# Token-routed attention block and expert layer: zero fill, one-hots, first block's root and third matrix moved within the prologue

## The chip, the cores and the metric

The kernel runs on one core of a Trainium2 chip. The metric is device time in microseconds (us), the median of three runs. Such a core has a matrix engine (TensorE, PE in the profile; its weight loads are shown as PEld), a vector engine (VectorE, DVE), a scalar engine (ScalarE, ACT), a programmable engine (GpSimd, POOL) and SyncE (SP), which in this kernel only issues transfers. Transfers run on 16 DMA engines; SyncE's go through queue q1, GpSimd's through queue q0.

## The reference

2048 tokens of 512 features pass through two layers. The first picks one of four 512x512 matrices by the token's number and uses that same matrix three times; the second is a mixture of 32 experts, of which every token takes four, with one shared expert.

```python
# first layer, xn = layernorm(x); C = ctx[e], e = token id // 6250
y   = (silu(xn @ C.T) * (xn @ C.T)) @ C
x   = x + y
# second layer
h   = rmsnorm(layernorm(x)) * norm_w
p   = top-4 of softmax(h @ gate_w.T), made to sum to 1
out = x + layernorm(x) + sum over the 4 experts of p * expert(h) + shared(h)
```

Both the expert and the shared path are `silu(h @ g) * (h @ u) @ d`. An expert holds at most 512 tokens.

## The kernel before

**Sorting the tokens.** The kernel first sorts the tokens by matrix, so that a block of 128 rows holds tokens of one matrix, or at a border is worked twice with a mask (`valid`). There are 16 blocks and up to 3 more at the borders (`XB` = 19). The sort is done with small matrix products: `ge` compares the token numbers with the borders (L226), `xm` is the membership (L229), and products with a triangular matrix count the ranks (L235 to L243). `split` cuts each token's place into block and row. Then, for each of 16 columns, `xa` is a one-hot of the row (L262), `xb16` is a one-hot of the block times the token's number (L253, L259), and 16 small matmuls add them up (L263). The result, `xtok` (L265), is the list of rows to gather. `planned` (L313) ends a chain of small VectorE instructions on which matrix each block uses.

**Gathering.** `x_block` (L332) is an indirect transfer that GpSimd issues, 128 rows of 2 KB each. GpSimd also computes the roots of the layer norm (`x_root`, L352, a power of -1/2), and the code ties its gathers and powers to a fixed order with `in_turn`: three gathers, then root 0, a gather, root 1, a gather, root 2, a gather, root 3, two gathers, the roots of blocks 4 to 7 in one, and eight gathers.

**One block.** VectorE takes mean and variance (`x_moments`, L344 and L345), GpSimd the root, VectorE two scalars (`x_norm`, L407 and L410), and ScalarE writes the normalised rows `hn` (L426). TensorE transposes them (`turn_block`), and the copy out of the accumulator is `xT`. `up` (L464) multiplies with the matrix, `gate` does silu(u)*u, and `down` (L485) multiplies with the same matrix again. For blocks after the first, `hold` (L395) lets ScalarE copy the block's matrix to a fixed place, because its number is known only at run time. TensorE's order in the steady part is: the next block's `up`, transposes of the block after, this block's `down`.

**The first block** is treated apart: VectorE and ScalarE each write half of `hn` (L416, L426), each half is transposed and copied by itself, and `up(0, ...)` goes by feature chunks, three before block 1's transposes and one behind. Idle matmuls (`turn_over`, L273) keep TensorE busy in the waits.

**Order.** The framework waits on data by itself; `behind` adds an order by hand, with a wait when it names `Sync`. `apart` states that two accesses don't touch. Every engine takes its own queue strictly in order. On VectorE the statistics of block 2 stand ahead of the copy `xT` of block 1, and those of block 3 ahead of block 0's gated product.

**Transfers from SyncE.** The token numbers, then three matrices of 1 MB (L111), the fourth after `planned`; behind the statistics of block 7 the weights of the second layer and 1 MB of zeros to the padding of the output (`second_inputs`, L133), and after the last gather 20.8 MB of blank rows to `s_dram` (L887). The zeros come from the tile `none` of 2084 columns, which GpSimd fills (L163) before writing an index into its last columns (L164).

The second layer (routing, scatter into `s_dram`, the experts' products, scatter into `out`) follows the first one's last blocks and is not touched.

Of the kernel before, what the change touches and what calls it, by code (L numbers as in the profile page):

```python
# [17 lines left out]
P = 128  # L18
T = 2048
D = 512  # L20
# [46 lines left out]
def tile_xattn_moe(  # L67
# [42 lines left out]
    def context(e):  # L110
        return nc.sync.dma_start(cT[:, e], ctxT[e].rearrange("(c p) f -> p c f", p=P))  # L111

    matrices = [context(e) for e in range(EX - 1)]
    gate_sb = const.tile([P, DC, E], F32, name="gate_sb")
    nw = const.tile([P, DC], F32, name="nw")
    nwq = const.tile([P, DC], F32, name="nwq")
# [31 lines left out]
    nc.vector.tensor_scalar(tri16, iota_q, row_b[:, 0:1], None, ALU.is_gt)  # L148
    iota16 = const.tile([P, P], F16, name="iota16")
    nc.vector.tensor_copy(iota16, iota_q)  # L150
    tok16 = const.tile([P, NT], F16, name="tok16")
    nc.vector.tensor_copy(tok16, tok1)
    ident = const.tile([P, P], F32, name="ident")
    at_hand = nc.vector.tensor_scalar(ident, iota_q, row_b[:, 0:1], None, ALU.is_equal)
    mhalf = const.tile([P, 2, GT], F32, name="mhalf")
# [4 lines left out]
    iota_e = const_iota([P, E], [[1, E]], "iota_e")  # L160

    spare = const_iota([P, NT, K], [[K * P, NT], [P, K]], "spare", base=NS, channel=1)
    nc.gpsimd.memset(none, 0.0)  # L163
# [60 lines left out]
    for e in range(1, EX):  # L224
# [20 lines left out]
    nc.vector.tensor_tensor(xv, px.rearrange("p (e t) -> p e t", e=EX), xm, ALU.mult)  # L245
    xrow = const.tile([P, NT], F32, name="xrow")
    nc.vector.tensor_reduce(xrow, xv.rearrange("p e t -> p t e"), AX.X, ALU.add)
    xblk, xq = split(xrow, ctx_pool, "x", F16)

    xa = ctx_pool.tile([P, NT, P], F16, name="xa")  # L250
    xbt = ctx_pool.tile([P, NT, NT], F16, name="xbt")
    xb16 = ctx_pool.tile([P, NT, NT], F16, name="xb16")
    nc.vector.tensor_tensor(  # L253
        xbt,
        iota16[:, :NT].unsqueeze(1).to_broadcast([P, NT, NT]),
        xblk.unsqueeze(2).to_broadcast([P, NT, NT]),
        ALU.is_equal,
    )
    nc.vector.tensor_tensor(xb16, xbt, tok16.unsqueeze(2).to_broadcast([P, NT, NT]), ALU.mult)  # L259
    pi = ps_s.tile([P, NT], F32, tag="sm", name="pi")  # L260
    for i in range(NT):
        nc.vector.tensor_scalar(xa[:, i, :], iota16, xq[:, i : i + 1], None, ALU.is_equal)  # L262
        nc.tensor.matmul(pi, xa[:, i, :], xb16[:, i, :], start=(i == 0), stop=(i == NT - 1))  # L263
    xtok = const.tile([P, NT], I32, name="xtok")
# [47 lines left out]
        nc.vector.scalar_tensor_tensor(valid, xw, xs_[:, e : e + 1], valid, ALU.is_ge, ALU.add)  # L312
    planned = nc.vector.tensor_tensor(valid, valid, be, ALU.is_equal)  # L313

    matrices.append(context(EX - 1))
    behind(matrices[-1], planned, mybir.DependencyClass.Sync)

# [49 lines left out]
    def x_registers(b):  # L367


        if b == 0:  # L370
            off[0] = 0
            regs[0] = 0, 0
            return None
        with queued(downs[-1] if downs else None):

            off[b] = nc.tensor.value_load(be_i[0:1, b : b + 1], min_val=0, max_val=min(b, EX - 1))
        with queued(adds_x[-1] if adds_x else halves[-1] if halves else None):
            dv = nc.vector.value_load(bl_i[0:1, b : b + 1], min_val=0, max_val=NT - 1)
            loaded = nc.cur_bb.bb.instructions[-1]
        with queued(reads[-1] if reads else None):  # L380
            ac = nc.scalar.value_load(bl_i[0:1, b : b + 1], min_val=0, max_val=NT - 1)
        regs[b] = dv, ac
        return loaded

    def hold(b):

        if b == 0:
            held[0] = cT[:, 0]
            return
        with queued(copies[-1] if copies else None):  # L390
            e = nc.scalar.value_load(be_i[0:1, b : b + 1], min_val=0, max_val=min(b, EX - 1))
        held[b] = ctx_pool.tile([P, DC, D], F32, tag="held", name=f"held{b}", bufs=2)
        n = DC // 2
        for h in range(0, DC, n):
            ins = nc.scalar.copy(  # L395
                held[b][:, h : h + n], cT[:, bass.ds(e, 1), h : h + n].rearrange("p o c f -> p (o c) f")
            )
            apart(ins, matrices[b + 1 :], "of experts that come later")
            copies.append(ins)

    def x_norm(b):
# [12 lines left out]
        n = D // 2 if b == 0 else 0  # L414
        if n:
            scaled = nc.vector.tensor_scalar(  # L416
                hn_[b][:, :n],
                acc[:, bass.ds(dv, 1), :n].rearrange("p o d -> p (o d)"),
                rv[:, 0:1],
                rv[:, 1:2],  # L420
                ALU.mult,
                ALU.add,
            )
            apart(scaled, loads[b + 1 :], "of blocks that come later")
            halves.append(scaled)
        ins = nc.scalar.activation(  # L426
            hn_[b][:, n:],
            acc[:, bass.ds(ac, 1), n:].rearrange("p o d -> p (o d)"),
            AF.Identity,
            bias=rv[:, 1:2],  # L430
            scale=rv[:, 0:1],
        )
# [26 lines left out]
    def up(b, fs, after_=None):  # L459
        if fs[0] == 0:  # L460
            ups[b] = ps_m.tile([P, DC, P], F32, tag="mm", name="pp")
        pairs = [(f, c) for f in fs for c in range(DC)] if b else [(f, c) for c in fs for f in range(DC)]
        for f, c in pairs:
            ins = nc.tensor.matmul(  # L464
                ups[b][:, f, :],
                held[b][:, c, f * P : (f + 1) * P],
                xT_[b][:, c, :],
                start=(f == 0 and c == 0) if b == 0 else (c == 0),
                stop=(c == DC - 1),
                skip_group_check=(b == 0),  # L470
            )
            if after_ is not None:
                behind(ins, after_)
        ups_.append(ins)

    def gate(b):
        s = xpool.tile([P, DC, P], F32, tag="s", name="s")
        gated.append(nc.scalar.activation(s, ups[b], AF.Silu))
        aT_[b] = xpool.tile([P, DC, P], F32, tag="aT", name="aT")
        made[b] = nc.vector.tensor_tensor(aT_[b], s, ups[b], ALU.mult)  # L480

    def down(b):
        po = ps_o.tile([P, D], F32, tag="po", name="po")
# [21 lines left out]
    def xattn():  # L505
        def fetched(*js):
            for j in js:
                x_block(j)

        fetched(0, 1, 2)  # L510
        for b in range(2):
            loaded = x_registers(b)
            with tc.issue_after(loaded) if loaded is not None else nullcontext():
                st = x_moments(b)
            behind(st, scaled if b else planned)
            if not b:
                turn_over(5, st)
            x_root(b)
            fetched(3 + b)
            scaled = x_norm(b)  # L520
            if b:
                behind(reads[-1], half_)
            else:
                xT_[0], half_ = turn_block(hn_[0], "xT", "xT", None)
        hold(0)
        up(0, range(DC - 1))
        hold(1)
        xT_[1] = turn_block(hn_[1], "xT", "xT", nc.vector, ups_[0])
        up(0, range(DC - 1, DC), turns[-1])
        gate(0)  # L530
        hold(2)
        for b in range(2, GT):
            st = x_moments(b)
            behind(st, turned[b - 2])
            behind(st, scaled)
            x_root(b)
            fetched(3 + b)
# [3 lines left out]
        for b in range(XB):  # L541
# [13 lines left out]
                hold(b + 2)  # L555
            if b + 1 < XB:
                up(b + 1, range(DC // 2))

            g, i = divmod(b - (XB - NT) - GT - 2, GT)
            if i == 0 and g >= 0:  # L560
# [845 lines left out]
```

## Time and profile before

| | before |
|---|---|
| median of 3 runs | 633.61 us (633.26 to 634.35) |
| the profiled execution's own time | 634.66 us |
| its span, first to last instruction | 632.8 us |
| mean granted TensorE clock | 0.99 |
| TensorE busy | 606.6 us, 96% |
| VectorE, ScalarE, GpSimd busy | 396.8, 216.6, 249.6 us |
| bytes moved by transfers | 144.55 MB, 228 GB/s |

All times in the views count from the span's first instruction. A row of the view in order of time has start, length, engine, line, operation, what it writes and reads, shapes, and in brackets the idle time before it with what ended it. The chain of waits has start, length and what; it goes from each piece of work back to what released it, so it holds only what set the end. "issue" there is time in which the engine waited for nothing that the profile shows. A queue's row has packets, MB and the time its packets took as a share of 16 engines. GpSimd's durations are rough; the distances between starts are better.

### The profile page before, as it was taken

How to read it: one execution, taken by the hardware profiler on the slowest of the kernel's cores; microseconds unless marked ns; L12 is line 12 of the kernel's file. 1: busy time of each engine (PE TensorE's matmuls, PEld its weight loads, DVE VectorE, ACT ScalarE, POOL GpSimd, SP SyncE). 2: the span in 40 equal slices, each digit the busy share in tenths (PEclk: the TensorE clock that was granted, in tenths of full speed). 3: DMA queues.
4: the chain of work that ended last, by engine and by line, in shares of the span. 5: the costliest groups of instructions: out<-in, count | busy, mean ns of one | idle time of the engine just before them, and what ended most of it. 6: DMA issues, size and time to landing. Idle time of an engine off the chain costs nothing.

```text
span 632.8 us, 10430 instructions
## 1 busy us (share of the span) xinstructions
PE 606.6 (96%) x2962; PEld 433.8 (69%) x2962; DVE 396.8 (63%) x1113; ACT 216.6 (34%) x390; POOL 249.6 (39%) x217
## 2 busy tenths in 40 slices
PE   5999999999996999999999999999999999999993
PEld 2777767777542444467687688858868886888882
DVE  7645457666734812675578577766766778677860
ACT  2444766665321000122233333332232333233330
POOL 4451111366673565424233235143332423434323
PEclk9999999999997999999999999999999999999998
DMA  7489992326273596799989998997999799999434
GB/s 253 147 316 416 412 415 100 136 103 221 102 270 118 175 392 210 212 299 291 299 209 273 275 258 199 276 249 155 288 257 256 168 266 250 246 251 217 52 48 56
DMA packets 104450, 144.55 MB, mean 228 GB/s; under 512 B 21184, under 2 KB 58048, under 8 KB 101824
## 3 DMA queue, kind: packets, MB, share of 16 engines
q1 hardware_dynamic: 86400, 101.54, 54.6%
q0 software_dynamic: 17984, 42.26, 27.5%
q8 instruction: 26, 0.43, 0.3%
q14 instruction: 40, 0.33, 0.2%
HBM read 79.05 MB, written 66.22 MB: 230 GB/s over the span
## 4 chain that ended last, share of the span: by engine, by line
PE 73%; POOL 8%; issue 7%; DVE 4%; DMA 4%; SPq 2%; another core or an unknown queue 1%; ACT 0%; POOLq 0%; DVEq 0%
PE pg L1068 17%; PE pu L1068 17%; PE po L1103 16%; PE pp L464 5%; POOL s_dram L652 4%; PE po L485 4%; PE pp_x L1150 3%; DMA acc<-in_x,xtok 3%; PE po L870 2%; PE pg L855 2%; PE po L1176 2%; SPq L940 2%; PE pu L855 2%; POOL rs L618 1%
## 5 line engine op out<-in xcount | busy, mean ns | idle before, releaser
L1040 POOL DMA_INDIRECT out<-eo,to_all x64 | 104.4, 1631 | 220.2 <-DVE eo L1109 87.2
L1068 PE MATMUL pg<-xT,w 128*128 128x256 f32 (+2 forms) x512 | 135.4, 377 | 0.0
L1106 ACT ACTIVATE eo<-po,wt 128x256 f32<-128x256 f32 x124 | 58.6, 475 | 172.8 <-PE po L1103 127.4
L1068 PE MATMUL pu<-xT,w 128*128 128x256 f32 (+2 forms) x512 | 114.0, 376 | 0.0
L1068 PEld LDWEIGHTS pg<-xT,w 128*128 128x128 f32 x512 | 96.6, 190 | 18.5 <-issue 6.2
L1068 PEld LDWEIGHTS pu<-xT,w 128*128 128x128 f32 x512 | 97.3, 190 | 11.5
L652 POOL DMA_INDIRECT s_dram<-h,slot x64 | 62.2, 971 | 35.2 <-issue 16.6
L464 PEld LDWEIGHTS pp<-xT,held 128*128 128x128 f32 x576 | 66.8, 192 | 7.6 <-issue 5.2
L464 PE MATMUL pp<-xT,held 128*128 128x128 f32 x576 | 68.2, 276 | 0.8 <-DVE st_b L611 0.6
L485 PE MATMUL po<-cT,aT 128*128 (+1 forms) x152 | 68.4, 592 | 0.0
L991 DVE STREAM_TRANSPOSE xT<-z 128x1024 f32<-128x1024 f32 x32 | 65.1, 2036 | 0.0
L1109 DVE SCALAR_TENSOR_TENSOR eo<-po,wt,eo 128x256 f32<-128x256 f32 x93 | 45.0, 484 | 18.6 <-PE po L1103 12.0
L1075 DVE TENSOR_TENSOR aT_r<-s,pu 128x256 f32<-128x256 f32 (+2 forms) x64 | 26.2, 414 | 43.0 <-PE pu L1068 37.2
L485 PEld LDWEIGHTS po<-cT,aT 128*128 128x128 f32 x152 | 27.4, 190 | 27.3 <-issue 27.3
L1001 ACT ACTIVATE xT<-xT,nwq 128x256 f32<-128x256 f32 x64 | 29.0, 500 | 44.6 <-DVE xT L991 32.7
L1086 DVE TENSOR_TENSOR t_r<-w,t_r 128x256 f32<-128x256 f32 x62 | 26.3, 424 | 28.0 <-PE po L1103 27.9
L618 POOL TENSOR_TENSOR rs<-rs,mhalf 128x2 f32<-128x2 f32 x16 | 11.3, 705 | 72.7 <-DVE rs L617 72.7
L1103 PE MATMUL po<-w,aT_r 128*128 128x256 f32 x124 | 39.8, 402 | 0.0
L395 ACT COPY held<-cT 128x1024 f32 x36 | 36.0, 1046 | 10.2 <-DVE valid L312 9.9
L1103 PE MATMUL po<-t_r,s_r 128*128 128x256 f32 x124 | 37.8, 386 | 0.3 <-DVE s_r L1093 0.3
L1103 PE MATMUL po<-t_r,aT_r 128*128 128x256 f32 x124 | 37.5, 384 | 0.0
L870 PE MATMUL po<-shw,aT_s 128*128 128x512 f32 x64 | 32.1, 640 | 1.5 <-issue 1.2
(203 smaller groups left out, 763.5 us busy)
## 6 DMA issues: line engine op xcount, KB each, us to landing
w<-in_w SPq DMA_DIRECT2D x192, 256.0 KB
s_dram<-none SPq DMA_DIRECT2D x1, 20840.0 KB
z<-s_dram SPq DMA_DIRECT2D x128, 128.0 KB
h_dram<-h SPq DMA_DIRECT2D x4, 1042.0 KB
cT<-in_ctxT SPq DMA_DIRECT2D x4, 1024.0 KB
out<-none SPq DMA_DIRECT2D x1, 1024.0 KB
s_dram<-h,slot POOLq DMA_INDIRECT x64
out<-eo,to_all POOLq DMA_INDIRECT x64
```

The source lines that it names most:

```text
L395: ins = nc.scalar.copy(held[b][:, h : h + n], cT[:, bass.ds(e, 1), h : h + n].rearrange("p o c f -> p (o c) f"))
L464: ins = nc.tensor.matmul(ups[b][:, f, :], held[b][:, c, f * P : (f + 1) * P], xT_[b][:, c, :], start=(f == 0 and c == 0) if b == 0 else (c ...
L485: ins = nc.tensor.matmul(po, aT_[b][:, f, :], cT[:, bass.ds(off[b], 1), f, :].rearrange("p o f -> p (o f)"), start=(f == 0), stop=(f == DC ...
L652: put = nc.gpsimd.indirect_dma_start(out=table, out_offset=bass.IndirectOffsetOnAxis(ap=index, axis=0), in_=src, in_offset=None,)
L870: ins = nc.tensor.matmul(po, aT[:, f, i * P : (i + 1) * P], w2t[:, f, :], start=(f == 0), stop=(f == IC - 1))
L991: ins = nc.vector.transpose(xT.rearrange("p c (r b) -> p r c b", b=SQ), z.rearrange("p r (a c) -> p r c a", c=DC))
L1001: nc.scalar.mul(xT[:, c, :], xT[:, c, :], nwq[:, c : c + 1])
L1040: put = nc.gpsimd.indirect_dma_start(out=out, out_offset=bass.IndirectOffsetOnAxis(ap=dst, axis=0), in_=eo, in_offset=None, bounds_check=T ...
L1068: last_up = nc.tensor.matmul(ps, w13t[:, c, f * P : (f + 1) * P], xT[:, c, :n], start=(c == 0), stop=(c == DC - 1))
L1103: return nc.tensor.matmul(ps, L[i], R[i], start=first_, stop=True, skip_group_check=True)
L1106: nc.scalar.mul(eo[i][:, j, :], ps, wt[:, i : i + 1])
L1109: return nc.vector.scalar_tensor_tensor(eo[i][:, j, :], ps, wt[:, i : i + 1], eo[i][:, j, :], ALU.mult, ALU.add)
```

## The change

It has four parts, all in the prologue.

1. The fill of `none` with zeros is now a multiplication by 0 on ScalarE. It uses another function than the Silu that ScalarE loads at the start, so a second table load stands behind it. GpSimd's index write into `none` waits for it.
2. The 16 columns of `xb16` are made one by one by GpSimd, each a comparison and a multiplication in one instruction, ahead of the matmul that reads it. `xbt`, `tok16` and the two wide VectorE instructions go; `xblk` is now kept in fp32.
3. Block 0 only has its mean taken off before the product (`x_centre`). Its product holds the rows of the block as the fixed operand and moves the matrix past them, 4 matmuls of 512 columns, so the result has tokens on partitions. The root times the mask (`x_scale`) is applied by the Silu's scale and in the gated product, which is then transposed (`turn_first`, 4 transposes and a ScalarE copy) halfway through block 1's product.
4. Only two matrices are requested at the start; the third is requested together with the fourth, after `planned`. ScalarE's copies for block 2 (`hold(2)`), which read the third matrix, are put behind its normalisation of block 1.

```diff
-    matrices = [context(e) for e in range(EX - 1)]
+    matrices = [context(e) for e in range(2)]
...
-    tok16 = const.tile([P, NT], F16, name="tok16")
-    nc.vector.tensor_copy(tok16, tok1)
...
-    nc.gpsimd.memset(none, 0.0)
+    nc.scalar.mul(none.rearrange("p j w -> p (j w)"), ones16[:, 0:1].to_broadcast([P, NB * RW]), 0.0)
...
-    xblk, xq = split(xrow, ctx_pool, "x", F16)
+    xblk, xq = split(xrow, ctx_pool, "x")
...
-    nc.vector.tensor_tensor(
-        xbt,
-        iota16[:, :NT].unsqueeze(1).to_broadcast([P, NT, NT]),
-        xblk.unsqueeze(2).to_broadcast([P, NT, NT]),
-        ALU.is_equal,
-    )
-    nc.vector.tensor_tensor(xb16, xbt, tok16.unsqueeze(2).to_broadcast([P, NT, NT]), ALU.mult)
     pi = ps_s.tile([P, NT], F32, tag="sm", name="pi")
     for i in range(NT):
+        nc.gpsimd.tensor_scalar(
+            xb16[:, i, :], iota16[:, :NT], xblk[:, i : i + 1], tok1[:, i : i + 1], ALU.is_equal, ALU.mult
+        )
...
-    matrices.append(context(EX - 1))
-    behind(matrices[-1], planned, mybir.DependencyClass.Sync)
+    for e in range(2, EX):
+        matrices.append(context(e))
+        behind(matrices[-1], planned, mybir.DependencyClass.Sync)
...
+    def x_centre():
+
+        regs[0] = 0, 0
+        off[0] = 0
+        neg = xpool.tile([P, 2], F32, tag="rv", name="rv", bufs=3)
+        nc.vector.tensor_scalar(neg[:, 0:1], xmv[:, 0, 0:1], -1.0, None, ALU.mult)
+        hn_[0] = xpool.tile([P, D], F32, tag="hn", name="hn")
+        n = D // 2
+        scaled = nc.vector.tensor_scalar(hn_[0][:, :n], acc[:, 0, :n], xmv[:, 0, 0:1], None, ALU.subtract)
+        halves.append(scaled)
+        reads.append(nc.scalar.activation(hn_[0][:, n:], acc[:, 0, n:], AF.Identity, bias=neg[:, 0:1]))
+        first_.append(neg)
+        return scaled
+
+    def x_scale():
+
+        ins = nc.vector.tensor_tensor(first_[0][:, 1:2], xr[:, 0:1], valid[:, 0:1], ALU.mult)
...
+                if b:
+                    ps, left, right = ups[b][:, f, :], held[b][:, c, f * P : (f + 1) * P], xT_[b][:, c, :]
+                else:
+                    ps, left, right = ups[b].rearrange("p f t -> p (f t)"), xT_[b][:, c, :], cT[:, 0, c, :]
+                ins = nc.tensor.matmul(ps, left, right, start=(c == 0), stop=(c == DC - 1))
...
+        by = first_[0][:, 1:2]
+        gated.append(nc.scalar.activation(s, ups[b], AF.Silu, scale=by))
+        made[b] = nc.vector.scalar_tensor_tensor(s, ups[b], by, s, ALU.mult, ALU.mult)
+        first_.append(s)
+
+    def turn_first(after_):
+        aT_[0] = turn_block(first_[1].rearrange("p f t -> p (f t)"), "aT", "aT", nc.scalar, after_)
...
+        st = x_moments(0)
+        behind(st, planned)
+        turn_over(5, st)
+        scaled = x_centre()
+        xT_[0], half_ = turn_block(hn_[0], "xT", "xT", None)
+        x_root(0)
+        fetched(3)
+        loaded = x_registers(1)
...
+        behind(x_scale(), powers[-1])
         up(0, range(DC - 1))
         hold(1)
...
         hold(2)
+        for ins in copies[2:]:
+            behind(ins, reads[-1])
...
+            if not b:
+                turn_first(ups_[-1])
```

More of the change, by code (lines that the diff above doesn't have):

```diff
@@ L247, in tile_xattn_moe @@
     nc.vector.tensor_reduce(xrow, xv.rearrange("p e t -> p t e"), AX.X, ALU.add)
-    xblk, xq = split(xrow, ctx_pool, "x", F16)
+    xblk, xq = split(xrow, ctx_pool, "x")
     xa = ctx_pool.tile([P, NT, P], F16, name="xa")
-    xbt = ctx_pool.tile([P, NT, NT], F16, name="xbt")
     xb16 = ctx_pool.tile([P, NT, NT], F16, name="xb16")
-    nc.vector.tensor_tensor(
-        xbt,
-        iota16[:, :NT].unsqueeze(1).to_broadcast([P, NT, NT]),
-        xblk.unsqueeze(2).to_broadcast([P, NT, NT]),
-        ALU.is_equal,
-    )
-    nc.vector.tensor_tensor(xb16, xbt, tok16.unsqueeze(2).to_broadcast([P, NT, NT]), ALU.mult)
     pi = ps_s.tile([P, NT], F32, tag="sm", name="pi")
     for i in range(NT):
+        nc.gpsimd.tensor_scalar(
+            xb16[:, i, :], iota16[:, :NT], xblk[:, i : i + 1], tok1[:, i : i + 1], ALU.is_equal, ALU.mult
+        )
         nc.vector.tensor_scalar(xa[:, i, :], iota16, xq[:, i : i + 1], None, ALU.is_equal)
@@ L367, in x_registers @@
     def x_registers(b):
[L370 to L373, printed above, removed]
         with queued(downs[-1] if downs else None):
@@ L385, in hold @@
     def hold(b):
-        if b == 0:
-            held[0] = cT[:, 0]
-            return
         with queued(copies[-1] if copies else None):
@@ L399, in hold @@
             copies.append(ins)
+    first_ = []
+    def x_centre():
[12 more added lines that the diff above has]
+        ins = nc.vector.tensor_tensor(first_[0][:, 1:2], xr[:, 0:1], valid[:, 0:1], ALU.mult)
+        powers.append(ins)
+        return ins
     def x_norm(b):
@@ L413, in x_norm @@
         hn_[b] = xpool.tile([P, D], F32, tag="hn", name="hn")
[L414 to L425, printed above, removed]
         ins = nc.scalar.activation(
-            hn_[b][:, n:],
-            acc[:, bass.ds(ac, 1), n:].rearrange("p o d -> p (o d)"),
+            hn_[b],
+            acc[:, bass.ds(ac, 1), :].rearrange("p o d -> p (o d)"),
             AF.Identity,
@@ L461, in up @@
             ups[b] = ps_m.tile([P, DC, P], F32, tag="mm", name="pp")
[L462 to L473, printed above, removed]
+        for f in fs:
+            for c in range(DC) if b else [f]:
+                if b:
[3 more added lines that the diff above has]
+                ins = nc.tensor.matmul(ps, left, right, start=(c == 0), stop=(c == DC - 1))
+                if after_ is not None:
+                    behind(ins, after_)
         ups_.append(ins)
@@ L477, in gate @@
         s = xpool.tile([P, DC, P], F32, tag="s", name="s")
-        gated.append(nc.scalar.activation(s, ups[b], AF.Silu))
-        aT_[b] = xpool.tile([P, DC, P], F32, tag="aT", name="aT")
-        made[b] = nc.vector.tensor_tensor(aT_[b], s, ups[b], ALU.mult)
+        if b:
+            gated.append(nc.scalar.activation(s, ups[b], AF.Silu))
+            aT_[b] = xpool.tile([P, DC, P], F32, tag="aT", name="aT")
+            made[b] = nc.vector.tensor_tensor(aT_[b], s, ups[b], ALU.mult)
+            return
+        by = first_[0][:, 1:2]
[4 more added lines that the diff above has]
+        aT_[0] = turn_block(first_[1].rearrange("p f t -> p (f t)"), "aT", "aT", nc.scalar, after_)
     def down(b):
@@ L510, in xattn @@
         fetched(0, 1, 2)
[L511 to L525, printed above, removed]
+        st = x_moments(0)
[6 more added lines that the diff above has]
+        loaded = x_registers(1)
+        with tc.issue_after(loaded):
+            st = x_moments(1)
+        behind(st, scaled)
+        x_root(1)
+        fetched(4)
+        scaled = x_norm(1)
+        behind(reads[-1], half_)
+        behind(x_scale(), powers[-1])
         up(0, range(DC - 1))
```

## The prediction

> **What bounds the kernel now.** I read the page first (TensorE busy for 606.6 us of the span), then the chain of waits over the first 110 us, because every edit lies before 30 us, then the instructions in order of time from 0 to 45 us, the DMA queues in slices of 1 us, and the groups of GpSimd.
>
> The page, then the chain of waits (start, length, what):
>
> ```profile
> PE 606.6 (96%) x2962; PEld 433.8 (69%) x2962; DVE 396.8 (63%) x1113; ACT 216.6 (34%) x390; POOL 249.6 (39%) x217
> ```
> ```profile
> 12.82 7.16 DMA acc<-in_x,xtok
> 20.00 0.71 DVE st_a L344
> ...
> 25.51 3.48 DMA acc<-in_x,xtok
> ...
> 35.76 6.83 DMA acc<-in_x,xtok
> ...
> 43.91 0.61 DVE xT L456
> 44.52 0.14 issue
> 44.66 3.81 PE pp L464 x32
> 48.47 0.44 PE tp L452 x4
> 48.90 3.44 PE po L485 x8
> ```
>
> The prologue is carried by gathered rows: the third gather (issued at 12.82, landed at 19.98) and those behind it. From 44.66 on TensorE runs without a gap. It had been continuous since 21.84 too, except for the 0.21 us it waited at 44.66 for the copy at 43.83. So two chains arrive together: the gathers decide by 0.21 us, TensorE is right behind. What moves the start of block 1's product at 21.84 moves the end by about as much.
>
> The instructions in order of time:
>
> ```profile
> 1.54 1.99 DVE L154 TENSOR_SCALAR ident<-iota_q,row_b 128x128 f32<-128x128 f32 x1
> 1.59 1.85 POOL L163 MEMSET none<- 128x2084 f32 x1
> 2.42 1.20 DVE L226 TENSOR_SCALAR ge<-tok_sb 128x16 f16<-128x16 int32 x3
> 5.94 0.42 DVE L253 TENSOR_TENSOR xbt<-iota,blk_x 128x256 f16<-128x256 f16 x1
> 6.78 2.52 DVE L262 TENSOR_SCALAR xa<-iota,row_x 128x128 f16<-128x128 f16 x15
> 9.59 0.17 DVE L265 TENSOR_SCALAR xtok<-pi 128x16 int32<-128x16 f32 x1 [0.29 <-PE pi L263]
> 12.12 0.18 DVE L313 TENSOR_TENSOR valid<-valid,be 128x19 f32<-128x19 f32 x1
> 21.10 0.69 DVE L456 COPY xT<-tp 128x512 f32<-128x512 f32 x1
> ```
>
> `ident` lasts as long as GpSimd's fill beside it; `ge` is caught behind it. `xtok`, the gather list, is ready 3.60 us after `row_x` (5.99). The copy `xT` of block 1 (21.10) stands on VectorE behind `st_a` of block 2, which waits for the third gather.
>
> The DMA queues from 16 to 17 us, while the last matrix flows (q1 carries SyncE's transfers, q0 the gathers):
>
> ```profile
> q1 hardware_dynamic: 191, 0.39, 104.3%
> q0 software_dynamic: 1, 0.00, 0.1%
> ```
>
> The gathers get nothing. A gather with the engines free (issued 25.51, landed 28.99) takes 3.48 us; the third took 7.16.
>
> **The change, part by part.**
>
> *Zero fill to ScalarE.* Removed: 1.85 us on GpSimd, and with it the block on `ident`. The token numbers are there at 2.42; three `ge` at 0.10 to 0.15 us end near 2.70, so `xm` starts at 2.72 and not 3.66: 0.94 us gained. Added on ScalarE: the fill, by its 256- and 512-element rows (0.60, 0.81, so 0.82 ns an element) 0.39+1.71 = 2.1 us from 2.03 to 4.1, and a second table load (1.28), done by 5.7. ScalarE is idle until 12.1 (9.95 us); that covers it. GpSimd's three small iotas now wait for the fill and end near 4.6, before the one-hots can start at 5.0; with that 0.4 us gone, each further tenth would delay them by a tenth.
>
> *Block one-hots to GpSimd.* VectorE loses `xbt`, `xb16` (0.38 and 0.34 on its path) and `tok16`. GpSimd gains 16 instructions of 128x16, and every one of the 16 small matmuls now waits for its own. The trace has none of this form. Lower bound: GpSimd's iotas start 0.105 apart, so VectorE's `xa` would pace it at 0.168. Upper: two-input GpSimd instructions take 0.567 us for 1 column and 1.026 for 4, both for a costly power; that line meets 0 columns at 0.41. Less the 0.1 that iotas overlap, 0.30 alone. `ident` shows that the two engines can exclude each other, so strict alternation would be 0.30+0.168 = 0.468. I take 0.30, nearest to the two-input rows and about the middle. Then `xtok` comes 16x0.30+0.39 = 5.2 us after `row_x`, 1.6 later than the 3.6 of before. With the 0.94 gained, `xtok` is 0.65 us late; at 0.168 it is 1.5 early, at 0.468 3.3 late.
>
> The Trainium skill, "SBUF — State Buffer", section "Who interferes with whom", says that a copy, cast or tensor_scalar of VectorE in a two-port mode and any GpSimd instruction lock each other out whole; `ident` (1.99 us beside the 1.85 us fill) agrees. By that rule alone the sum below would be +6.2.
>
> *Third matrix later.* SyncE now requests 1 MB twice, not once, after `planned`; nothing else stands on its queue until 29.7. The last matrix, requested at 12.32, flowed from 14.3 to 17.7, and the third gather's rows moved only after 17.3. A second megabyte at the 0.39 MB/us seen takes 2.6 us. The first gather gains nothing: it took 3.6 us against 3.48 with free engines. The second is under way when the flow starts and keeps its time. The third lands at worst 2.6 us later relative to `xtok`; at best, if the queues alternate, not later. I take 2.6: in the slice above the gathers get 0.1%, and that is the nearest row. Third matrix's own reader, `hold(2)`, runs behind block 1's normalisation (20.4) and has its data by about 19.5.
>
> The Trainium skill, "DMA: Bandwidth & Descriptors", section "Queues, rings and completion order", has an engine alternate between its queues packet by packet. The slice from 16 to 17 us speaks against it at this grain. By the rule the 2.6 falls away and the sum is about +1.
>
> *Root behind the product.* Block 0's rows no longer wait for GpSimd's power (0.58) and two small VectorE steps: `hn` starts about 1.1 us earlier after `st_a`. But block 0's product (24 matmuls to 20.2) ends beside block 1's own chain, which is second gather 16.87, root 18.55, `hn` 19.54, transposes 20.41: nothing of it reaches 21.84. The new first product, 4 matmuls of 512 columns (8 passes, 3.44 by the `po` row), replaces 32 passes at 3.7. Added on TensorE's continuous path: 4 transposes inside block 1's product, 0.44. They wait for VectorE's `s`, queued behind block 3's statistics; counted from the third gather's landing it ends at 3.7, the transposes come up at 3.65: 0.1 of stall. ScalarE's copy of them (0.6) ends 1.5 us before `down(0)` needs it. `hold(2)`'s two copies (2.1) now precede block 0's Silu on ScalarE, hidden in the wait for the third gather; without it they cost 0.2. One gain: the root of block 3 leaves ahead of `s`, so gathers 7 and 8 are some 0.6 earlier; the gathers stop being last at up(4) and TensorE's own 0.21 of slack is used.
>
> **Sum.** +0.65 (`xtok`) +2.6 (matrix) +0.44 +0.1 -0.21 = +3.6. The profiled execution took 634.66 (span 632.8 and 1.9 around it), 1.05 above the median of three, 633.61; the shift is put on the median: **637.2 us**.
>
> **Rivals.**
> - *GpSimd at VectorE's pace* (0.168): `xtok` 1.5 early, sum +1.4, 635.0. For it: iotas 0.105 apart. Against: they read nothing.
> - *Lock-step alternation* (0.468): +6.2, 639.9. For it: `ident`. Against: the casts at 1.12 to 1.54 lost only hundredths beside iotas.
> - *The gathers aren't held* by the second megabyte: sum +1.0 at 0.30, 634.6. This one turns "not slower" when GpSimd's pitch is under 0.24 us, and ends at -1.2 (632.4) at 0.168. For it: from 37.3 to 44.5 gathers and the store of zeros share the engines. Against: the slice shown, and that the ninth gather, issued at 31.91, moved only when most of the shared weights were in (36.5).
> - *The late stall moves.* At 188.7 TensorE and ScalarE stop for 7 us on no wait that the trace shows (8.42 on "another core or an unknown queue" in the chain), and the clock is 0.50 from 194 to 200. The order and number of instructions ahead of it change. If it dissolves, the time falls by up to 7.1 and about 2 for the clock, and the change ends faster, near 630, once more than 3.6 of it goes; a new one of that kind would give about 644. Against: three runs within 0.2% show that it is steady.
>
> While TensorE waits some 2.7 us for the third gather its clock could drop; the 4.7 us stop at 191.3 did that. I price it at 0, at most 2 us.
>
> **How the numbers follow.** Main case (held, 0.22 to 0.40) 0.47: 635.9 to 639; GpSimd fast 0.15; lock-step 0.10; gathers free 0.17, half of it within 0.2%, the rest slower but for 0.02; stall gone 0.11. A measurement of this kernel tells about 0.2% (1.27 us) from no change. Faster 0.13, same 0.10, slower 0.77. The range, from 632.4 (gathers free, GpSimd fast) to 640.0 (lock-step), leaves out the stall and part of lock-step.
>
> **What would show it.** `ident` near 0.3 us and `xm` near 2.7; GpSimd's 16 one-hots 0.30 apart with matmuls waiting for them, `xtok` near 10.2; the third gather landing near 23.2, q0 empty for about 4 us; block 1's product near 25; four transposes in it, and up(4) at 48.2 without a wait for a gather. It is wrong if the third gather lands before 21, if the one-hots are under 0.2 us apart, or if the stop at 188.7 has another length.

## The result and the profile after

| | before | after |
|---|---|---|
| median, 6 runs each | 633.98 us (633.26 to 635.16) | 638.01 us (636.76 to 638.75) |
| ratio | | 1.0059, 95% interval 1.0046 to 1.0072 |
| profiled execution: own time, span | 634.66, 632.8 us | 638.53, 636.8 us |

The changed kernel is 0.59% slower, some 3.7 us (the two medians lie 4.0 apart). The forecast was 637.2, within 632.4 to 640.0. The total came out by luck: two of the terms behind it were wrong by 2.0 and 2.7 us, in opposite directions, and nearly cancelled.

The first lines of the page after, TensorE as the bound as before:

```profile
PE 608.2 (96%) x2942; PEld 432.2 (68%) x2942; DVE 395.0 (62%) x1110; ACT 220.2 (35%) x393; POOL 252.4 (40%) x232
```

The view in order of time of the kernel after, 0 to 13 us (start, length, engine, line, operation, count, and in brackets the idle time before and what ended it):

```profile
1.47 0.28 DVE L152 TENSOR_SCALAR ident<-iota_q,row_b 128x128 f32<-128x128 f32 x1
2.04 1.94 ACT L161 ACTIVATE none<-ones 128x2084 f32<-128x2084 f16 x1
2.76 0.19 DVE L227 TENSOR_TENSOR xm<-ge 128x64 f16<-128x64 f16 x1
3.99 1.28 ACT L157 ACT_TABLE_LOAD   x1
...
4.92 0.17 DVE L198 CAST row_x<-vi 128x16 f32<-128x16 int32 x1
5.12 6.93 POOL L252 TENSOR_SCALAR xb<-iota,blk_x,tok 128x16 f16<-128x16 f16 x16 [0.58 <-DVE row_x L198]
5.12 2.90 DVE L255 TENSOR_SCALAR xa<-iota,row_x 128x128 f16<-128x128 f16 x16
...
11.70 0.17 PE L256 MATMUL pi<-xb,xa 128*128 128x16 f16 x1 [0.23 <-POOL xb L252]
12.10 0.17 PE L256 MATMUL pi<-xb,xa 128*128 128x16 f16 x1 [0.23 <-POOL xb L252]
12.31 0.17 DVE L258 TENSOR_SCALAR xtok<-pi 128x16 int32<-128x16 f32 x1 [4.29 <-PE pi L256]
```

`ident` takes 0.28 instead of 1.99 us, and `xm` starts at 2.76 instead of 3.66: the fill's 0.9 is there. Then more is lost than was won. VectorE's 16 `xa` are done at 8.02, GpSimd's 16 `xb` only at 12.05; the small matmuls come 0.40 apart behind them, VectorE sits idle for 4.29 us, and the gather list `xtok` is ready at 12.31 instead of 9.59.

The chain of waits of the kernel after, 18 to 50 us (start, length, what):

```profile
18.77 6.36 DMA acc<-in_x,xtok
25.13 0.03 issue
25.16 0.07 DVE st_a L338
...
26.38 0.67 DVE s L479
27.05 0.04 issue
27.09 0.66 PE tp L449 x4
27.75 1.79 PE pp L465 x16
29.54 0.44 PE tp L449 x4
29.97 3.43 PE po L488 x8
33.41 3.57 PE pp L465 x32
```

The transfer on the chain is another one than before. It is the fourth gather (issued 18.77, landed 25.13, 6.36 us; before 15.68 and 4.95 us). The statistics of block 3 (`st_a`) wait for it, VectorE's `s` stands behind them, and TensorE's four new transposes wait for `s`, in the middle of block 1's product. From 27.09 on TensorE sets the order, but for a gap of 0.42 at 46.15 for which no wait is shown.

The rows in order of time on which the steps below rest; first the products of blocks 1 and 2 in the kernel before, then in the kernel after the statistics behind the third gather, block 1's product (two halves), the transposes between them and block 2's product:

```profile
21.84 3.84 PE L464 MATMUL pp<-xT,held 128*128 128x128 f32 x32
29.39 3.73 PE L464 MATMUL pp<-xT,held 128*128 128x128 f32 x32
...
22.66 0.69 DVE L338 BATCH_NORM_STATS2 st_a<-acc 128x6 f32<-128x512 f32 x1 [1.26 <-DMA acc<-in_x,xtok]
24.42 2.05 PE L465 MATMUL pp<-xT,held 128*128 128x128 f32 x16 [0.59 <-DVE xT L453]
27.09 0.66 PE L449 MATMUL tp<-ident,s 128*128 128x128 f32 x4 [0.63 <-DVE s L479]
33.25 3.73 PE L465 MATMUL pp<-xT,held 128*128 128x128 f32 x32
```

The DMA queues of the kernel after in slices of 1 us, 18 to 19, 19 to 20, 20 to 21, 22 to 23 and 23 to 24 (q1 SyncE's transfers, q0 gathers; packets, MB, share):

```profile
q1 hardware_dynamic: 192, 0.39, 102.4%
q0 software_dynamic: 11, 0.01, 2.5%
...
q1 hardware_dynamic: 189, 0.39, 101.5%
...
q0 software_dynamic: 56, 0.22, 53.8%
q1 hardware_dynamic: 110, 0.20, 52.6%
...
q1 hardware_dynamic: 196, 0.40, 103.5%
q0 software_dynamic: 2, 0.00, 1.1%
...
q1 hardware_dynamic: 123, 0.24, 63.0%
q0 software_dynamic: 44, 0.18, 43.8%
```

The first of the two megabytes has the engines to itself, as the one did before; then gathers get about half of them; then the second megabyte has them, and gathers again. From 17 to 21 us q1 moved 1.08 MB (0.10, 0.39, 0.39, 0.20 in the four slices), so the gathers' stretch falls where the first matrix ends. So the third gather waits for one megabyte, as before (10.33 us after `xtok`, before 10.39), and the fourth waits for the other.

Step by step, in the two profiles: `xtok` is 2.72 late. Block 1's product starts 2.58 late (21.84, 24.42). From there to block 2's product it takes 8.83 us instead of 7.55, 1.28 more: the transposes 0.66 and the wait before them 0.63. That makes 3.86 (29.39, 33.25), and the seventh `down` product is 3.99 late (71.94, 75.93). The span ends 4.0 late. Between these, three things that the edit doesn't name nearly cancel: about 0.6 of further lag up to 172 us, 0.4 at the late stop, and 1.0 less between TensorE's last product and the end (10.1, 9.1).

### The profile page after: what moved, and what is told of

Same layout as the page of the kernel before. It is cut to its first block, busy times and chain, and to the rows that moved or that the text cites. A ratio compares the mean times of both kernels' runs of the same rounds, so it can differ in the third digit from the quotient of the medians.

```text
span 636.8 us, 10406 instructions
## 1 busy us (share of the span) xinstructions
PE 608.2 (96%) x2942; PEld 432.2 (68%) x2942; DVE 395.0 (62%) x1110; ACT 220.2 (35%) x393; POOL 252.4 (40%) x232
## 4 chain that ended last, share of the span: by engine, by line
PE 73%; issue 7%; POOL 6%; DMA 4%; SPq 2%; DVE 2%; another core or an unknown queue 1%; POOLq 1%; ACT 0%; DVEq 0%
PE pg L1076 17%; PE pu L1076 16%; PE po L1111 15%; PE po L488 6%; PE pp L465 6%; POOL s_dram L660 4%; PE pp_x L1158 3%; PE po L878 2%; PE pg L863 2%; SPq L948 2%; PE po L1184 2%; PE pu L863 2%; DMA out<-eo,to_all 2%; DMA acc<-in_x,xtok 1%
## 5 line engine op out<-in xcount | busy, mean ns | idle before, releaser
L1048 POOL DMA_INDIRECT out<-eo,to_all x64 | 101.9, 1592 | 221.1 <-DVE eo L1117 118.5
```

What stands on the lines that cost most here:

```text
L1048: put = nc.gpsimd.indirect_dma_start(out=out, out_offset=bass.IndirectOffsetOnAxis(ap=dst, axis=0), in_=eo, in_offset=None, bounds_check=T ...
```

## The experiments

Twelve kernels ran, in three groups of four. Each group ran on one chip, the three on three different ones, and is compared with the kernel before on the same chip; which chip the first comparison above ran on isn't known. In the groups the kernel before takes 625.1 to 625.6 us; what is missing there against 634 us is shown with the runs of both kernels. The absolute times in the first group's expectations are on the scale of 634 us, and are read as differences.

The table has, for each, when `xtok` starts, how long after it the third and fourth gathers have landed, the starts of the products of blocks 1 and 2, the end of TensorE's last product (one profile each, us), and the ratio of times to before. Rows are named as below.

| kernel | `xtok` | third | fourth | block 1 | block 2 | TensorE's end | ratio (95%) |
|---|---|---|---|---|---|---|---|
| before_again | 9.59 | 11.19 | 11.84 | 22.56 | 30.11 | 614.3 | 1.0005 (0.9994 to 1.0016) |
| after_again | 12.37 | 10.53 | 12.97 | 24.68 | 33.45 | 617.5 | 1.0040 (1.0025 to 1.0056) |
| a_vec | 8.86 | 10.56 | 13.16 | 21.20 | 30.15 | 614.2 | 1.0002 (0.9990 to 1.0013) |
| a_third | 12.39 | 10.67 | 11.29 | 24.84 | 32.82 | 616.9 | 1.0027 (1.0017 to 1.0037) |
| a_root | 12.36 | 10.57 | 12.65 | 25.97 | 33.52 | 617.5 | 1.0034 (1.0023 to 1.0044) |
| a_half | 9.81 | 10.87 | 12.98 | 22.46 | 30.91 | 614.9 | 1.0011 (1.0001 to 1.0020) |
| a_late | 8.74 | 7.02 | 12.79 | 20.20 | 29.65 | 613.7 | 1.0005 (0.9994 to 1.0015) |
| b_pool | 13.12 | 10.89 | 11.51 | 25.78 | 33.33 | 618.0 | 1.0031 (1.0020 to 1.0042) |
| b_fill | 8.91 | 11.06 | 11.53 | 21.75 | 29.30 | 613.3 | 0.9989 (0.9979 to 1.0000) |
| b_third | 9.59 | 11.12 | 13.36 | 23.43 | 30.98 | 615.5 | 1.0006 (0.9992 to 1.0019) |
| b_root | 9.59 | 10.99 | 11.62 | 22.35 | 30.34 | 614.9 | 1.0007 (0.9995 to 1.0020) |
| b_fill_late | 8.68 | 6.98 | 10.13 | 21.45 | 29.00 | 613.9 | 0.9996 (0.9985 to 1.0007) |

One caution on the last two columns. Between TensorE's last product and the span's end lay 8.3 to 11.4 us in these profiles, with GpSimd's last two stores in it; the last was issued 1.3 us behind that product in `a_third`, 3.2 in `a_vec`. That spread is as large as the smaller effects, and rows of different groups come from different chips. So the ratio says what a kernel is worth, and the columns on TensorE say what the prologue did.

**The one-hots back on VectorE** (`a_vec`), from the kernel after:

```diff
-        nc.gpsimd.tensor_scalar(xb16[:, i, :], iota16[:, :NT], xblk[...], tok1[...], ALU.is_equal, ALU.mult)
+    nc.vector.tensor_tensor(xbt, iota16..., xblk..., ALU.is_equal)       # both wide, ahead of the loop
+    nc.vector.tensor_tensor(xb16, xbt, tok16..., ALU.mult)
```

> The changed kernel with the block one-hots back on VectorE. Theory now (the one-hots' own pace on GpSimd, 0.40 us each, carries most of it): xtok at about 8.7 instead of 12.31, and all that follows it 3.6 us earlier; the third gather again some 10.3 after xtok, the stall for s stays; time about 634.4, within 0.5 us of before. Rival (the prediction's step: the one-hots cost 1.6 and a second megabyte ahead of the third gather 2.6): third gather 12 us or more after xtok once the list is early, time about 636.4.

`xtok` came at 8.86, 3.51 earlier than in `after_again`, and the whole loss was gone: block 2's product 3.30 earlier, the time that of before. The third gather stayed at 10.56 after `xtok`. The rival would have kept 2.4 us of the loss.

**The one-hots on GpSimd alone** (`b_pool`), the same edit made to the kernel before:

> The kernel before with the block one-hots on GpSimd alone. Theory now (own pace 0.40, 0.43 to 0.55 beside VectorE's one-hots): xtok at about 13.2 instead of 9.59, every later step 3.6 later, time about 637.5. Rival (the prediction's pitch of 0.30): xtok at 11.2, time about 635.5. Rival (the pace is an exclusion between the two engines): as soon as VectorE's xa have ended, the pitch falls well under 0.40.

The view in order of time of `b_pool`:

```profile
6.01 6.84 POOL L252 TENSOR_SCALAR xb<-iota,blk_x,tok 128x16 f16<-128x16 f16 x16 [2.22 <-DVE row_x L198]
6.02 2.84 DVE L255 TENSOR_SCALAR xa<-iota,row_x 128x128 f16<-128x128 f16 x16
13.12 0.17 DVE L258 TENSOR_SCALAR xtok<-pi 128x16 int32<-128x16 f32 x1 [4.26 <-PE pi L256]
```

`xtok` at 13.12 is 3.53 late, as the theory had it. From 8.87 on, when VectorE's `xa` had all ended or were ending, the rest of the sixteen started 0.40 apart. So 0.40 is GpSimd's own pace; up to there the starts are 0.41 to 0.59 apart, 0.48 in the mean, so VectorE beside it adds some 0.08 to each. The time rose by 0.31%, 1.9 us, less than TensorE's 3.6, for the reason given with the table.

**Every other column on VectorE** (`a_half`), which asks whether the two engines exclude each other:

```diff
-        nc.gpsimd.tensor_scalar(xb16[:, i, :], ...)
+        eng = nc.gpsimd if i % 2 else nc.vector
+        eng.tensor_scalar(xb16[:, i, :], ...)
```

> The changed kernel with every other block one-hot on VectorE (the same form there), eight left on GpSimd. Theory now (GpSimd's own pace, 0.40 an instruction, beside a VectorE that keeps 0.17 an instruction): 24x0.17+0.4 = 4.5 after row_x on VectorE, 8x0.45 = 3.6 on GpSimd, so xtok at about 9.7 instead of 12.3 and the time 2.6 to 2.8 under the changed kernel. Rival (the two engines exclude each other instruction by instruction): 24x0.17+8x0.40 = 7.3 after row_x, xtok at about 12.4, no gain.

The view in order of time of `a_half`:

```profile
5.24 3.98 POOL L253 TENSOR_SCALAR xb<-iota,blk_x,tok 128x16 f16<-128x16 f16 x8 [0.71 <-DVE row_x L198]
...
8.93 0.32 DVE L253 TENSOR_SCALAR xb<-iota,blk_x,tok 128x16 f16<-128x16 f16 x1
9.12 0.40 DVE L256 TENSOR_SCALAR xa<-iota,row_x 128x128 f16<-128x128 f16 x2
...
9.81 0.17 DVE L259 TENSOR_SCALAR xtok<-pi 128x16 int32<-128x16 f32 x1 [0.29 <-PE pi L257]
```

`xtok` at 9.81, not 12.4: VectorE did its 24 at 0.17 to 0.18 each while GpSimd did its eight in 3.98, 0.50 each, in the same time. Exclusion instruction by instruction is refuted for these forms; a drag on GpSimd of 0.1 an instruction is what remains of it. The two aren't independent either: GpSimd's last five starts are 0.52 apart, just as long as three instructions of VectorE take here. What couples them stays open. The time, 1.0011, kept about a quarter of the kernel after's loss (1.0040).

**The third matrix at the start again** (`a_third`), from the kernel after:

```diff
-    matrices = [context(e) for e in range(2)]
+    matrices = [context(e) for e in range(EX - 1)]
-    for e in range(2, EX):
+    for e in range(EX - 1, EX):
```

> The changed kernel with the third matrix requested at the start again. Theory now: the third gather does not move (10.3 to 10.4 after xtok), the fourth lands about 11 after xtok instead of 12.8, TensorE's wait for s inside block 1's product (0.63) goes; time 0.6 to 0.9 under the changed kernel, about 637.2. Rival (the second megabyte holds the third gather): third gather 2.6 earlier, time 2.6 under the changed kernel, about 635.4.

The third gather didn't come earlier (10.67 after `xtok`, `after_again` 10.53). The fourth did, by 1.7, and the wait for `s` went. Block 2's product is 0.63 earlier, TensorE's end 0.7. The prediction's step is refuted, and the trace bears out the new one. The time alone wouldn't show it: the ratios 1.0027 and 1.0040 have intervals that overlap.

**The third matrix later, alone** (`b_third`), the same edit reversed, in the kernel before:

> The kernel before with the third matrix requested behind planned, alone. Theory now: the third gather still lands about 10.4 after xtok; the fourth at 12.7 instead of 11.0; but ScalarE's fourth copy into held, at 17.53 before, now waits for the third matrix until about 19.4 and stands ahead of block 1's hn (19.54), so that block 1's product starts 0.5 to 1.5 later than 21.84 and the time is about 1 above before. The prediction's step (third gather held by a second megabyte): third gather at about 22.6, time 2.6 above before. Third possibility: nothing moves, time as before.

The view in order of time of `b_third`:

```profile
20.17 1.04 ACT L396 COPY held<-cT 128x1024 f32 x1 [2.90 <-DMA cT<-in_ctxT]
20.74 0.69 DVE L345 BATCH_NORM_STATS2 st_a<-acc 128x6 f32<-128x512 f32 x1 [0.89 <-DMA acc<-in_x,xtok]
21.12 0.81 ACT L427 ACTIVATE hn<-acc,rv 128x512 f32 x1
...
23.43 3.84 PE L465 MATMUL pp<-xT,held 128*128 128x128 f32 x32
```

The third gather landed 11.12 after `xtok`; `before_again` has 11.19 without the edit. What came late was ScalarE: its copy of the third matrix now waited 2.90 us for it, ahead of block 1's `hn`, and block 1's product started 0.87 later than in `before_again`. The time, 1.0006, can't be told from before, where about 1 us more was expected. In the kernel after that copy is held behind `hn` (the order that stands with the third matrix in the list of the change; `b_third` ran without it, `b_root` with it), so the same transfer costs there what it does to the fourth gather.

**Block 0's root ahead of its product again** (`a_root`), and **the root behind it, alone** (`b_root`):

```diff
-        scaled = x_centre()              # after: subtract the mean, root and mask go into gate(0)
+        x_root(b)                        # before: root, scale and shift, then the transposes
+        scaled = x_norm(b)
-                turn_first(ups_[-1])     # after: four transposes of s within block 1's product
```

> The changed kernel with block 0 normalised before its product again (root, scale and shift ahead of the transposes; no transposes of s). Theory now: the four transposes (0.44) and the wait for s behind the fourth gather (0.63 to 0.9) go, block 1's product starts where it did (about 24.4), time 1.1 to 1.4 under the changed kernel, about 636.7. Rival (the root's place had earned something on block 0's path): block 1's product starts up to 1.1 later, time equal or up to 0.5 above the changed kernel.

> The kernel before with block 0's root applied behind its product, alone (with its transposes of s and ScalarE's copies held back behind the rows' reads). The prediction's step: four more transposes, 0.44, and at most 0.1 of wait for s, less 0.21 of slack: time 0.3 above before. Theory now adds: with the fourth matrix alone the fourth gather lands about 11 after xtok, s waits for nothing, block 2's product starts within 0.3 of 29.39 and the gap at 44.66 closes: time within 0.4 of before. Rival (the root's place itself costs block 1's start): block 1's product later than 22.3, time 0.7 or more above before.

`a_root` missed: block 1's product started 1.3 later than in `after_again`, at 25.97, not where it did. Most of the reason is in the view in order of time of `a_root`:

```profile
22.71 1.04 ACT L389 COPY held<-cT 128x1024 f32 x1 [2.62 <-DMA cT<-in_ctxT]
23.67 0.81 ACT L420 ACTIVATE hn<-acc,rv 128x512 f32 x1
```

It is `b_third`'s wait again, on a `hn` whose scalars were there at 22.80: 0.87 of the 1.3. The scalars themselves came 1.00 later than in `after_again` (21.80), 0.69 of it because the second gather landed later; no run shows whether the root's place has a part in that. This run undid two things at once, the root and the order that kept this copy out of the way, so what it says of the root alone is little. `b_root` says it better: block 1's product 0.21 earlier than in `before_again`, as much as the third gather landed earlier (10.99 after `xtok` for 11.19); four transposes 0.44, block 2's product 0.23 later, no wait for `s`. The time, 1.0007, can't be told from before. The two profiles are from two chips, so tenths are their limit.

**The zero fill on ScalarE alone** (`b_fill`):

```diff
-    nc.gpsimd.memset(none, 0.0)
+    nc.scalar.mul(none..., ones16[:, 0:1].to_broadcast([P, NB * RW]), 0.0)
```

> The kernel before with the zero fill on ScalarE alone. The prediction's step: ident near 0.3, xm at 2.7 to 2.8 instead of 3.66, xtok at about 8.7 and everything behind it 0.8 to 0.9 earlier, time 0.8 under before. Rival (the first gather now meets the third matrix, which lands until 12.2, and gains nothing): first gather at 13.2 or later, time within 0.5 of before.

`xm` at 2.97, `xtok` at 8.91, 0.68 earlier. The first gather landed at 13.39, only 0.34 earlier than in `before_again`, so half of that gather's gain was lost, which fits the rival's collision with the third matrix (landed 12.12): in `a_vec`, where that matrix is requested later, a first gather issued at 9.34 took 3.70 us, while this one, issued at 9.38, took 4.01. The second came 0.85 earlier. Block 2's product is 0.81 earlier, TensorE's end 1.1. The time fell by 0.11%, with an interval that ends at no change: the only part that shows a gain.

**Both kernels again on these chips** (`after_again`, `before_again`):

> The changed kernel as it is, on the chip of this comparison, where the kernel before took 625.4 us and no stop near 190 us appeared in four variants. By the theory now the change's cost lies before 50 us and is the same with or without that stop: block 2's product starts 3.9 later than before, the last work of TensorE ends some 4 later. If the stop is a property of the chip and not of the kernel, the trace shows none here. A rival (the change's cost depends on the stop): ratio to before clearly under 1.003.

> The kernel before as it is, traced on the chip of these comparisons. Theory now: no stop near 190 us here; TensorE's last product ends about 613.9; the third gather lands 10.4 to 11 after xtok, as in the variants that request three matrices at the start. If the stop is a property of the program and not of the chip, the trace shows it again.

The view in order of time of `before_again`:

```profile
22.56 3.84 PE L464 MATMUL pp<-xT,held 128*128 128x128 f32 x32 [0.43 <-DVE xT L456]
...
189.01 1.12 PE L870 MATMUL po<-shw,aT_s 128*128 128x512 f32 x2
189.97 0.27 PE L683 MATMUL pl<-ident,lT 128*128 128x128 f32 x1
```

In the profile of before that the prediction used, the matmul `pl` came at 196.00, behind a stop of 4.7 us; here it follows at once. None of the twelve profiles has that stop. The chain of waits of the kernel after, in the first comparison, has it:

```profile
191.91 8.46 another core or an unknown queue
```

The same program has it in one comparison and not in the others, so it isn't set by the program alone; what it is stays open. It lies behind most of the difference between 634 and 625 us: TensorE's last product ends 8.35 earlier here, and 6.03 of that are there at `pl`. The change's cost doesn't hang on it: +0.40% here, +0.59% there, with intervals that overlap. In `before_again` block 1's product is itself later (22.56 for 21.84), because its third gather lands 11.19 after `xtok` and not 10.39, and the change then costs 3.34 at block 2's product instead of 3.86 (one profile each, from two chips).

**Two attempts at a better kernel.** Both request the last matrix only behind block 1's statistics, so that no matrix flows while the first three gathers do; `a_late` on top of `a_vec` with the third matrix at the start, `b_fill_late` on top of `b_fill`:

```diff
-    behind(matrices[-1], planned, mybir.DependencyClass.Sync)
+        behind(matrices[-1], st, mybir.DependencyClass.Sync)   # in xattn, st = statistics of block 1
```

> The changed kernel with the one-hots on VectorE, the third matrix at the start and the last matrix requested only behind block 1's statistics (root and fill stay as changed). Theory now: no matrix flows while the first three gathers do, so the second lands about 1 and the third some 3 earlier (7 to 8 after xtok), s waits for nothing, block 1's product starts near 20.4 instead of 21.84, and the time is 0.8 to 1.5 under before. Rival (the later gathers or the last matrix, met by each other, take it back before block 4): block 2's product no earlier than 29.0, time within 0.4 of before.

> The kernel before with the zero fill on ScalarE and the last matrix requested only behind block 1's statistics. Theory now: the third gather lands 7 to 8 after xtok instead of 11, but block 1's product is bound by TensorE's own work since block 0's product starts (17.03 with the fill alone, 4.5 before block 1's), so it gains only 0.1 to 0.3 over the fill alone; time 0.6 to 1.0 under before. Rival (the gathers bind after all): block 1's product a microsecond or more earlier than with the fill alone.

In both the third gather landed 7.0 us after `xtok`. In `a_late` block 1's product started at 20.20, 2.4 earlier than before. Then the view in order of time shows the price:

```profile
21.56 0.69 DVE L342 BATCH_NORM_STATS2 st_a<-acc 128x6 f32<-128x512 f32 x1 [1.41 <-DMA acc<-in_x,xtok]
23.50 0.66 PE L453 MATMUL tp<-ident,s 128*128 128x128 f32 x4 [1.24 <-DVE s L483]
```

The fourth gather, issued at 15.61, now met the matrix requested at 15.96; `s` waited for it as in the kernel after, 1.24 us. Block 2's product came at 29.65, 0.46 early, and the time is that of before: the rival. In `b_fill_late` block 1's product gained 0.30 over `b_fill`, as expected, and TensorE lost 0.6 at 44.05, waiting for an `xT` that stood behind the statistics of a later gather. Neither beats `b_fill`.

The two differ in where block 0's root stands (one-hots on VectorE and the fill on ScalarE in both). With it behind the product, block 1's product starts 1.25 earlier (20.20 for 21.45), and the last matrix is requested 1.25 earlier too (15.96, 17.21), before the fourth gather's rows have moved; that gather lands 2.7 later after `xtok`, and block 2's product starts 0.65 later.

## Why the prediction was right in its total and wrong in its terms

| term | predicted | measured, first comparison |
|---|---|---|
| zero fill, `xm` earlier | -0.94 | -0.90 |
| one-hots | +1.6 (0.30 each) | +3.62 (0.40 each, more beside VectorE) |
| third gather behind the second megabyte | +2.6 | -0.06 |
| four transposes of `s` | +0.44 | +0.66 (0.43 where `s` is ready) |
| wait for `s` | +0.1 | +0.63 |
| slack at block 4 | -0.21 | -0.21, and a new gap of 0.42 at 46.15 |
| rest | | -0.09 |
| block 2's product (without the slack) | | +3.86 |

- **Zero fill:** right, mechanism and size. ScalarE's fill took 1.94 us (2.1 predicted) and the second table load ended at 5.27, ahead of all that needs ScalarE; `b_fill` alone gives the gain.
- **One-hots:** the mechanism was right, every small matmul waiting for its own, and the size of the term was off by 2.0. The step that failed is "less the 0.1 that iotas overlap, 0.30 alone". GpSimd's iotas start closer together than they last; these instructions do so hardly at all (a median of 0.43 long, 0.40 apart). The row from which the bound came, the power's line to 0 columns at 0.41, was right as it stood; that is one agreement, and no run shows that a power and a comparison have the same fixed part. The rival of alternation had the nearer number (`xtok` 3.3 late; it was 2.7), but `a_half` refutes its mechanism. The Trainium skill, "SBUF — State Buffer", section "Who interferes with whom", has a `tensor_scalar` of VectorE in a two-port mode and a GpSimd instruction lock each other out whole. That is borne out by `ident` (1.99 us beside the fill, 0.28 without it) and not by these small forms; whether they run in such a mode no run here shows.
- **Third matrix:** the step that failed is "I take 2.6". It read the slice from 16 to 17 us, in which gathers got nothing, as a queue that holds gathers for as long as it has work. In the kernel after it held them for one megabyte, and the third gather moved before the second. `a_third`, `b_third` and both kernels agree that the second megabyte doesn't move that gather. How the queues share isn't always so clean: in `b_third` both moved side by side from 18 to 21 us (q1 71 to 80%, q0 23 to 25%). One megabyte already explains 3.5 to 4.1 us of the third gather's time (7.02 after `xtok` in `a_late` for 10.56 in `a_vec`, 6.98 in `b_fill_late` for 11.06 in `b_fill`), so the first of them was priced in before. The Trainium skill, "DMA: Bandwidth & Descriptors", section "Queues, rings and completion order", which the prediction set aside, has the queues take turns by packets. A packet is there a batch of some 9 to 17 descriptors, so turns by it can be long, and the slice from 16 to 17 us, whose packets are of 2 KB, didn't speak against it as the prediction had it. The runs agree that there are turns, in stretches of a microsecond or more (q1 102.4% beside q0 2.5%, later 52.6% beside 53.8%); where a packet of the page ends no run shows. By it the prediction's third rival would have been the main case, and, with the one-hots at 0.30, the total +1.0 where +3.7 was measured.
- **What the megabyte did hold:** the fourth gather. The step that failed is the count of `s` "from the third gather's landing": the prediction named that `s` is queued behind block 3's statistics, but not that these wait for a gather with another landing time. 0.63 of wait instead of 0.1, gone in `a_third` and in `b_root`. There block 2's product follows block 1's by 7.98 and 7.99 us instead of 7.55, so the four transposes cost 0.43 to 0.44, as priced; the other 0.2 of the table's 0.66 comes with the wait.
- **Root behind the product:** right that nothing of block 0's head start reaches block 1's product while the third gather is late, whose statistics stand ahead of `xT` (`b_root`); with an early third gather it does (20.20 in `a_late`, 21.45 in `b_fill_late`).
- **The stop near 190:** stayed as priced, 8.46 for 8.42, and is absent elsewhere in both kernels alike. The three runs that the prediction took to show it steady were runs of one comparison.

Parts measured alone, at block 2's product against `before_again`: -0.81, +3.22, +0.87 and +0.23 make +3.51; together they cost +3.34. The one-hots are nearly all of it. That the sums agree so well is in part chance: the +0.87 comes from a copy ahead of `hn`, which the kernel after keeps out of the way, while it has the fourth gather's wait instead; and the profiles are from three chips.

## What to carry to other kernels

Count a train of small instructions by a start-to-start distance of the same kind of instruction; where the trace has none, take the nearest rows as they stand: here the two-input rows came near the pace, and the correction taken from another kind of row spoilt it. When a second transfer is put behind a first, ask which of the waiting transfers it meets and not whether the queue is full: here the third gather paid nothing and the fourth did, and what waited in the end was an engine two steps behind. A total that fits proves none of its terms; only taking each part away showed that one was 2 us too small and one 2.7 too large.

## What the runs showed of the hardware that was not expected

- Two megabytes requested back to back on q1 left the gathers on q0 about half of the engines' time where the first ended (53.8% from 20 to 21 us, after 2.5% and less in the two microseconds before).
- GpSimd's compare-and-multiply on 128x16 starts every 0.40 us alone, 0.48 to 0.50 beside a busy VectorE, which itself keeps 0.17 to 0.18 an instruction.
- The stop of 4.7 to 5.2 us near 190 us was in both profiles of the first comparison and in none of the twelve later ones, on three chips; the same kernel before took 634 us there and 625 us here.
- From TensorE's last product to the end the same ending took 8.3 to 11.4 us in these profiles, which hides or doubles an effect of a microsecond in the time.
